# Sigmoid by way of the hyperbolic tangent, and one-number activations beside the square root, in a four-layer graph network

## The chip, the cores and the metric

The kernel runs on one core of a Trainium2 chip. The core has engines that work side by side, each with its own queue of instructions in a fixed order: TensorE (PE, matrix products), VectorE (DVE), ScalarE (ACT, functions and copies), GpSimd (POOL) and SyncE (SP, which here only issues transfers). The metric is device time in microseconds (us) from start to end; lower is better. Three runs of the kernel before took 5743.28, 5758.06 and 5765.65 us; their median, 5758.06 us, is the time before.

## The reference, cut to what matters

There are 16 graphs of 1024 nodes with 64 numbers a node, and an adjacency matrix of 1024 x 1024 each. Four layers follow one another. Each is a residual step that begins with a normalization without learned scale, clipped at zero:

```python
def _layernorm(x, axis=-1, eps=1e-5):
    m = jnp.mean(x, axis=axis, keepdims=True)
    v = jnp.var(x, axis=axis, keepdims=True)
    return (x - m) / jnp.sqrt(v + eps)

h = jnp.maximum(_layernorm(x, axis=-1), 0.0)
x = x + _L0_gnn_ref(h, adj, nodemask, ...)   # quantiles over the neighbours, then a small dense net
# layer 1: message net, A @ m, then a gated update
r = jax.nn.sigmoid(i_r + h_r)
z = jax.nn.sigmoid(i_z + h_z)
n = jnp.tanh(i_n + r * h_n)
return (1.0 - z) * n + z * h
# layer 2: A @ h, dense, tanh, dense        -> x + tanh(...) @ W2 + b2
# layer 3: attention over columns, softmax, weighted sum, relu
```

So one graph needs the square root once at each of four normalizations, the sigmoid and the hyperbolic tangent in layer 1, the hyperbolic tangent in layer 2 and the exponential in layer 3. All of these run on ACT, which evaluates functions from a table that has to be in place. In the trace a change of table is an instruction of its own, ACT_TABLE_LOAD.

## The kernel before, in words

Graphs are worked on in eight pairs. The four layers of the reference are spread over stages, which repeat from pair to pair with a period of some 695 us:

- **Sorting and neighbours.** `sort_begin` (L750) loads the two graphs' node features (`xt`, a buffer of the name `s4` with three places), normalizes them (`norm`, L705, under the name `so`) and transposes them; `sort_pair` (L778) sorts each channel on DVE and works the ranks backwards; `prepare` (L1617) calls `neighbours` (L882), which reads the adjacency, thins out the edges and writes a transposed copy of the adjacency to HBM (`a_d`).
- **Selection.** `weights` (L984) and `select` (L1105) find the quantiles of layer 0, for both graphs of the pair, with matrix products, sign functions and maxima. No square root, tangent or exponential occurs there.
- **Leftovers.** `extras` (L1325) treats the rows that the selection could not settle.
- **Layers.** `layers` (L1398) does the rest of layer 0 and layers 1 to 3 for one graph. It is called for both graphs of the pair (names `ly0` and `ly1`), and each call contains three normalizations under the name `ly`.

While the layers of one pair run, `prepare` and `sort_pair` for the next pair, and `sort_begin` for the pair after that, are offered beside them. In the last pair there is nothing to put beside the layers.

The order on each engine's queue is not written by hand. A planner takes the instructions in the order in which the program states them as their rank, walks through a modelled time with its own costs, and at each moment gives an engine the highest-ranked instruction that is ready in that model. So the first graph's layers rank above the second's, both above `prepare` and `sort_pair`, and `sort_begin` ranks last. The queue that comes out is fixed: on the chip an engine whose next instruction waits does not go on to a later one. The table loads are put in afterwards, when the queue's order is known: one stands ahead of each activation whose function the table in place does not serve.

The parts that the change touches:

- In `norm`, DVE takes statistics of each group of 64 numbers (L710) and combines them (L712), eight groups for a graph, sixteen for a pair; ACT takes the square root into `sd` (L714); DVE inverts it (L716), subtracts the mean (L718), and clips and scales (L720). L718 does not need `sd`, L716 and L720 do.
- In `layers`, the gates of layer 1 are made for two node groups at a time: PE writes the products to a bank of PSUM (L1535), ACT takes the sigmoid of the first two gates into `rz` (L1540), DVE multiplies the first gate into the candidate's hidden part and adds the input part (L1542, L1543). After four such rounds ACT takes the hyperbolic tangent of all candidates (L1544), and four DVE instructions blend it with `h1` and add the residual (L1546 to L1549).
- Layer 2 takes its hyperbolic tangent at L1560. Layer 3 loops over eight blocks of the adjacency: a scaled copy on ACT (L1587), a minimum on DVE (L1589) with two one-column helpers (L1592, L1593), the exponential on ACT (L1595), a masked sum on DVE (L1596), a scaling of the features on ACT (L1601), and the product on PE (L1485). The exponentials are written to `att`, which has two places.

Of the kernel before, what the change touches and what calls it, by code (L numbers as in the profile page):

```python
# [9 lines left out]
F32 = mybir.dt.float32  # L10
# [7 lines left out]
AF = mybir.ActivationFunctionType  # L18
ALU = mybir.AluOpType
# [23 lines left out]
def gnn_stack(ctx, tc, x, adj, nodemask, w, out):  # L43
# [10 lines left out]
    nc = tc.nc  # L54
    B, N, C = x.shape
# [17 lines left out]
    eps = const.tile([P, 1], F32, name="eps")  # L73
# [630 lines left out]

    def norm(pool, big, xt, g, name):  # L705

        st = pool.tile([P, g, 6], F32, name=f"{name}_st")
        mv = pool.tile([P, g, 2], F32, name=f"{name}_mv")
        for t in range(g):
            nc.vector.bn_stats(st[:, t, :], xt[:, t, :])  # L710
        for t in range(g):
            nc.vector.bn_aggr(mv[:, t, :], st[:, t, :])  # L712
        sd = pool.tile([P, g], F32, name=f"{name}_sd")
        nc.scalar.activation(sd, mv[:, :, 1], AF.Sqrt, bias=eps, scale=1.0)  # L714
        rs = pool.tile([P, g], F32, name=f"{name}_rs")
        nc.vector.reciprocal(rs, sd)  # L716
        d = big()
        nc.vector.tensor_sub(d, xt, mv[:, :, 0:1].to_broadcast([P, g, C]))  # L718
        h = big()
        nc.vector.scalar_tensor_tensor(  # L720
            h, d, 0.0, rs.rearrange("p (g o) -> p g o", o=1).to_broadcast([P, g, C]), op0=ALU.max, op1=ALU.mult
        )
        return h
# [674 lines left out]
    def layers(b, side_, agg, ly, lb, held=None):  # L1398
# [5 lines left out]
        def nd(name, bufs=1):  # L1404
            return ly.tile([P, NT, C], F32, name=name, bufs=bufs)

        def big():
            return nd("nd", 4)
# [4 lines left out]
        def bank():  # L1413
            return lb.tile([P, HALF], F32, name="bank")
# [31 lines left out]
        def add_row(po, row_3):  # L1446

            n = row_3.shape[1]
            nc.tensor.matmul(
                po.rearrange("p (t c) -> p t c", c=n), ones_3,  # L1450
                row_3.rearrange("k (o c) -> k o c", o=1).to_broadcast([3, HALF // n, n]), start=True, stop=False,
            )
# [60 lines left out]


        h1 = norm(ly, big, x1, NT, "ly")
        hT = transposed(h1, "hT")
        both_ = ly.tile([P, 2, HALF], F32, name="two")
# [11 lines left out]
        rz = ly.tile([P, N], F32, name="att", bufs=2).rearrange("p (t k) -> p t k", k=2 * C)  # L1529
        nn = big()  # L1530
        for g in range(0, NT, 2):
            pg = bank()
            add_row(pg, gates_3)
            for f in range(2):
                nc.tensor.matmul(  # L1535
                    pg[:, f * 4 * C : (f + 1) * 4 * C], both_[:, f, g // 2 * P : (g // 2 + 1) * P], gates[:, f, :],
                    start=False, stop=(f == 1),
                )
            pg = pg.rearrange("p (t k) -> p t k", k=4 * C)
            nc.scalar.activation(rz[:, g : g + 2, :], pg[:, :, : 2 * C], AF.Sigmoid)  # L1540
            rn = ly.tile([P, 2, C], F32, name="rn", bufs=2)
            nc.vector.tensor_mul(rn, rz[:, g : g + 2, :C], pg[:, :, 3 * C :])  # L1542
            nc.vector.tensor_add(nn[:, g : g + 2, :], rn, pg[:, :, 2 * C : 3 * C])  # L1543
        nc.scalar.activation(nn, nn, AF.Tanh)  # L1544
        x2 = nd("xs", 2)
        nc.vector.tensor_sub(x2, h1, nn)  # L1546
        nc.vector.tensor_mul(x2, x2, rz[:, :, C:])
        nc.vector.tensor_add(x2, x2, nn)
        nc.vector.tensor_add(x2, x2, x1)  # L1549


        h2 = norm(ly, big, x2, NT, "ly")
        h2T = transposed(h2, "srcT")
        pm = bank()
# [90 lines left out]
    for pr in range(pairs):  # L1645
# [17 lines left out]
        with ExitStack() as beside:  # L1663
# [14 lines left out]
            with (  # L1678
                tc.tile_pool(reuse_waits="tile", name="ly0", bufs=1) as ly0,
                tc.tile_pool(reuse_waits="tile", name="ly1", bufs=1) as ly1,  # L1680
                tc.tile_pool(reuse_waits="tile", name="lb0", bufs=4 if final else 3, space=PSUM) as lb0,
                tc.tile_pool(reuse_waits="tile", name="lb1", bufs=4 if final else 2, space=PSUM) as lb1,
                ExitStack() as besides,
            ):
                if not final:
                    sop = besides.enter_context(tc.tile_pool(reuse_waits="tile", name="sop", bufs=1, space=PSUM))
                for i, (ly, lb) in enumerate(((ly0, lb0), (ly1, lb1))):
                    layers(pr * 2 + i, (pr * 2 + i) % 4, aggs[i], ly, lb, held[i])
                if pr + 1 < pairs:
                    made = prepare(pr + 1, nb, nbp)  # L1690
                    sort_pair(pr + 1, cur, sop)
                if pr + 2 < pairs:
                    cur = sort_begin(pr + 2, sop)
# [47 lines left out]
```

## Time and profile before

| | |
|---|---|
| median of three runs | 5758.06 us |
| the profiled execution, its own time | 5775.25 us |
| its span | 5773.4 us |
| busy: DVE / PE / ACT | 4997.9 / 4354.5 / 3813.2 us |
| table loads on ACT | 91, of 1283 ns each |
| square roots (L714) | 56: 8 of `so`, 48 of `ly` |
| a selection stage, 2382 to 2763 us | DVE 355.3, PE 329.2, ACT 279.7 us busy of 381 |
| a stage of leftovers, layers and sorting, 2062 to 2382 us | DVE 263.4, PE 214.1, ACT 197.7 us busy of 320 |
| last layers alone, 5597 to 5773.4 us | PE 118.6, DVE 83.0, ACT 79.1 us busy of 176.4 |

The times are from one execution recorded by the hardware profiler. "Busy" leaves out register, branch, semaphore and transfer-issuing instructions. In lists of groups a line gives source line, engine, operation, output<-input by the program's names, shapes and count, then the total busy time and the mean of one instruction in nanoseconds, and last the engine's idle time just before these instructions with what ended it. The chain of waits is followed back from the last instruction: at each step to what released it or to the instruction before it on its engine; its lines give start, duration, engine, output and source line, and "issue" is time in which an engine waited for nothing that the profile shows. A table load has no output, so in the chain it appears as an engine and a line alone, or inside an "issue".

### The profile page before, as it was taken

Reading aid. Unit: us, or ns where it says so; the run is one execution under the profiler, and the core shown is the slowest. Engines: PE = TensorE matmul, PEld = TensorE weight load, DVE = VectorE, ACT = ScalarE, POOL = GpSimd, SP = SyncE. Lnnn points to the kernel's source line nnn. Section 1 sums busy time; section 2 is a strip of 40 time slices with the busy share of each in tenths; the row PEclk is TensorE's granted clock in tenths of the full one; section 3 lists DMA queues with packets and bytes.
Section 4 is the critical chain, followed back from the end, with each engine's and each line's share of the span. In section 5 each row is a group of like instructions: output and inputs, shape, how many; then the busy total and the mean of one; then the engine's idle time right before and its main releaser. Section 6 shows DMA issues by size and latency. Waiting matters only on the chain.

```text
span 5773.4 us, 114332 instructions
## 1 busy us (share of the span) xinstructions
PE 4354.5 (75%) x45010; PEld 2724.9 (47%) x45010; DVE 4997.9 (87%) x13239; ACT 3813.2 (66%) x5763; POOL 166.5 (3%) x292
## 2 busy tenths in 40 slices
PE   1488677886778957788588885788767886779956
PEld 1355443554435544455434554355543554435642
DVE  9899888998889987999879988799888998878754
ACT  2587657775586855868568666687667866477835
POOL 3000000000000000000000000000000000000000
PEclk9699878997789978899779996899868997789967
DMA  4401264013731047210561115611255013630030
GB/s 129 127 27 41 88 208 134 26 37 107 227 96 35 28 133 232 68 37 23 158 225 53 41 45 175 199 38 40 82 173 173 28 40 90 212 113 18 10 101 5
DMA packets 519813, 551.45 MB, mean 96 GB/s; under 512 B 263297, under 2 KB 413057, under 8 KB 519265
## 3 DMA queue, kind: packets, MB, share of 16 engines
q1 hardware_dynamic: 376864, 459.65, 25.5%
q10 hardware_dynamic: 140064, 81.84, 4.6%
q8 instruction: 355, 5.82, 0.4%
q0 software_dynamic: 2336, 2.57, 0.2%
q14 instruction: 194, 1.58, 0.1%
HBM read 360.17 MB, written 183.76 MB: 94 GB/s over the span
## 4 chain that ended last, share of the span: by engine, by line
PE 34%; DVE 32%; ACT 19%; DMA 10%; issue 4%; POOL 0%; SPq 0%; ACTq 0%; DVEq 0%; POOLq 0%
PE comb L1120 11%; ACT sign L1175 6%; DVE y L1191 5%; PE cand L1220 5%; PE comb L1311 3%; PE bank L1485 3%; DVE cand L1228 3%; DMA a_d<-at 2%; ACT y L1128 2%; DVE cum L902 2%; DMA adjT<-a_d 2%; DVE s L793 1%; DVE s L792 1%; PE pk L952 1%; DVE swapped L791 1%
## 5 line engine op out<-in xcount | busy, mean ns | idle before, releaser
L1120 PE MATMUL comb<-wt,ndT 128*128 128x512 fp8e5 x6144 | 1435.6, 385 | 136.3 <-ACT sign L1175 112.1
L1128 ACT ACTIVATE y<-comb,qb 128x512 int16<-128x512 f32 x1152 | 743.5, 711 | 497.2 <-PE comb L1120 497.2
L1120 PEld LDWEIGHTS <-ndT 128*128 128x128 fp8e5 x6144 | 589.3, 98 | 852.9 <-issue 222.2
L1175 ACT ACTIVATE sign<-comb,lower 128x1024 fp8e5<-128x1024 int16 (+1 forms) x640 | 694.1, 1085 | 0.0
L1175 ACT ACTIVATE sign<-comb,half 128x1024 fp8e5<-128x1024 int16 (+1 forms) x640 | 688.9, 1076 | 0.0
L1220 PE MATMUL cand<-vtab,sign 128*128 128x48 f16 (+1 forms) x18432 | 668.4, 191 | 25.1 <-DVE agg L1097 15.2
L1220 PEld LDWEIGHTS <-sign 128*128 128x128 fp8e5 x18432 | 641.7, 96 | 85.1 <-issue 23.9
L1191 DVE TENSOR_TENSOR y<-y 128x512 uint16<-128x512 uint16 (+5 forms) x896 | 670.1, 790 | 10.5 <-PE comb L1173 10.0
L1228 DVE COPY_PREDICATED cand<-w_f,cand 128x256 f32<-128x256 uint16 (+1 forms) x1536 | 532.7, 378 | 84.1 <-PE cand L1220 81.7
L1173 PE MATMUL comb<-ident_b,y 128*128 128x128 bf16 x4608 | 307.0, 218 | 102.2 <-ACT sign L1175 70.2
L910 ACT COPY at<-pk 128x512 f32<-128x512 f32 x256 | 147.2, 585 | 351.6 <-PE pk L908 177.2
L952 PE MATMUL pk<-minus_b,rem 128*128 128x128 bf16 x1024 | 231.4, 251 | 175.6 <-ACT rem L933 175.6
L1173 PEld LDWEIGHTS <-y 128*128 128x128 bf16 x4608 | 284.8, 97 | 127.2 <-issue 127.1
L952 PE MATMUL pk<-ident_b,ni 128*128 128x128 bf16 x1024 | 227.0, 247 | 108.0 <-ACT ndT L958 63.4
L902 DVE TENSOR_TENSOR_SCAN cum<-ni 128x1024 f16<-128x1024 fp8e5 x128 | 292.3, 2284 | 17.7 <-POOL ni L898 14.4
L1485 PE MATMUL bank<-att,hs 128*64 128x512 f32 x512 | 195.7, 876 | 143.5 <-ACT hs L1601 143.5
L908 PE MATMUL pk<-ident,a 128*128 128x128 f32 x1024 | 188.0, 330 | 144.8 <-DMA a<-in_adj_dram 92.0
L998 DVE TENSOR_SCALAR wt<-node 128x2048 uint8<-128x2048 f16 x224 | 263.3, 1219 | 21.9 <-PE comb L1311 21.9
L1485 PE MATMUL bank<-adjT,nd 128*64 128x512 f32 x896 | 255.5, 638 | 29.7 <-DMA adjT<-a_d 29.2
L792 DVE TENSOR_TENSOR s<-s 128x384 f32<-128x384 f32 (+4 forms) x440 | 263.2, 598 | 0.0
L793 DVE TENSOR_TENSOR s<-s 128x384 f32<-128x384 f32 (+4 forms) x440 | 262.1, 596 | 0.0
L1186 DVE TENSOR_SCALAR y<-y 128x4608 int16<-128x4608 int16 x128 | 173.6, 1356 | 97.6 <-ACT y L1128 96.7
(382 smaller groups left out, 8340.5 us busy)
## 6 DMA issues: line engine op xcount, KB each, us to landing
adjT<-a_d SPq DMA_DIRECT2D x336, 512.0 KB
a<-in_adj_dram SPq DMA_DIRECT2D x128, 512.0 KB
a_d<-at ACTq DMA_DIRECT2D x256, 256.0 KB
m_d<-swapped SPq DMA_DIRECT2D x104, 512.0 KB
swapped<-m_d SPq DMA_DIRECT2D x104, 512.0 KB
n_d<-nat SPq DMA_DIRECT2D x128, 128.0 KB
x_d<-xr SPq DMA_DIRECT2D x48, 256.0 KB
comb_x<-x_d ACTq DMA_DIRECT2D x24, 512.0 KB
```

The lines of the kernel that those rows point to most:

```text
L792: nc.vector.tensor_tensor(to_lo, lo, hi, op=ALU.max)
L793: nc.vector.tensor_tensor(to_hi, lo, hi, op=ALU.min)
L902: nc.vector.tensor_tensor_scan(cum[:, t - t0, :], ni[:, t, :], wide[:, t, pad - 1 : pad - 1 + N], 0.0, op0=ALU.add, op1=ALU.add)
L952: nc.tensor.matmul(pk[:, n % 4, :], lhs, rhs, start=(n % 4 == 0 and m == 0), stop=(m == len(terms) - 1 and last),)
L1120: nc.tensor.matmul(pw, ndT[:, j, t * P : (t + 1) * P], wt[1 + g8][:, j].rearrange("p w c -> p (w c)"), start=(j == 0), stop=(j == NT - 1),)
L1128: nc.scalar.activation(y[:, 0, chunks, at : at + 8 * d_].rearrange("p q (w d) -> p q w d", d=d_), pw.rearrange("p (w q d) -> p q w d", w=8 ...
L1173: nc.tensor.transpose(pt[:, q - q0, :], y[:, 0, q, :].bitcast(BF16), ident_b)
L1175: nc.scalar.activation(signs[tl][s][:, q0:q1, :], pt.bitcast(I16), AF.Sign, bias=before[s], scale=-1.0, saturate=False,)
L1191: nc.vector.tensor_tensor(v[:, :, :, :n], v[:, :, :, :n], v[:, :, :, n : 2 * n], op=ALU.max)
L1220: nc.tensor.matmul(cand[:, e, at : at + 12 * d_].rearrange("p (d l) -> p d l", l=12), signs[tl][sec][:, chunk, :], tab[:, q, :, half_ * 12 ...
L1228: nc.vector.copy_predicated(v[:, :, :, dst : dst + k], mk.to_broadcast([P, 2, C // 2, k]), v[:, :, :, frm : frm + k])
L1485: nc.tensor.matmul(po[to : to + C, :], lhs, rhs[:, f * HALF : (f + 1) * HALF], start=(j == 0), stop=(j == NT - 1))
```

## The change

The sigmoid is written as half of one plus the hyperbolic tangent of half the argument. ACT now computes the tangent with a scale of 0.5 at L1540, and `rz` holds the tangents. The half and the one go into the DVE instructions that follow: two `tensor_tensor` forms at L1542 and L1543 become `scalar_tensor_tensor` (add one, multiply; multiply by a half, add), and two of the four that blend (L1547, L1548) likewise. The number of DVE instructions stays what it was.

In `norm` two ACT instructions on a single number are added, with results that nothing reads, in a tile `turn` of one partition and two numbers. The first is a square root (scale 0, so that its value doesn't depend on its input); it reads the first number of `xt` and stands ahead of the statistics. The second is an exponential, also with scale 0; it reads the first number of `sd` and stands right after the square root. This concerns all 56 normalizations, in `sort_begin` and in `layers`.

```diff
     def norm(pool, big, xt, g, name):
 
+        turn = pool.tile([1, 2], F32, name=f"{name}_turn")
+        nc.scalar.activation(turn[:, :1], xt[:1, 0, :1], AF.Sqrt, bias=eps[:1], scale=0.0)
         st = pool.tile([P, g, 6], F32, name=f"{name}_st")
...
         sd = pool.tile([P, g], F32, name=f"{name}_sd")
         nc.scalar.activation(sd, mv[:, :, 1], AF.Sqrt, bias=eps, scale=1.0)
+        nc.scalar.activation(turn[:, 1:], sd[:1, :1], AF.Exp, scale=0.0)
         rs = pool.tile([P, g], F32, name=f"{name}_rs")
...
-            nc.scalar.activation(rz[:, g : g + 2, :], pg[:, :, : 2 * C], AF.Sigmoid)
+            nc.scalar.activation(rz[:, g : g + 2, :], pg[:, :, : 2 * C], AF.Tanh, scale=0.5)
             rn = ly.tile([P, 2, C], F32, name="rn", bufs=2)
-            nc.vector.tensor_mul(rn, rz[:, g : g + 2, :C], pg[:, :, 3 * C :])
-            nc.vector.tensor_add(nn[:, g : g + 2, :], rn, pg[:, :, 2 * C : 3 * C])
+            nc.vector.scalar_tensor_tensor(rn, rz[:, g : g + 2, :C], 1.0, pg[:, :, 3 * C :], op0=ALU.add, op1=ALU.mult)
+            nc.vector.scalar_tensor_tensor(
+                nn[:, g : g + 2, :], rn, 0.5, pg[:, :, 2 * C : 3 * C], op0=ALU.mult, op1=ALU.add
+            )
         nc.scalar.activation(nn, nn, AF.Tanh)
         x2 = nd("xs", 2)
         nc.vector.tensor_sub(x2, h1, nn)
-        nc.vector.tensor_mul(x2, x2, rz[:, :, C:])
-        nc.vector.tensor_add(x2, x2, nn)
+        nc.vector.scalar_tensor_tensor(x2, rz[:, :, C:], 1.0, x2, op0=ALU.add, op1=ALU.mult)
+        nc.vector.scalar_tensor_tensor(x2, x2, 0.5, nn, op0=ALU.mult, op1=ALU.add)
         nc.vector.tensor_add(x2, x2, x1)
```

## The prediction

> **What bounds the kernel now.** I read the page first, then the busy times by stage, then the table loads among ACT's groups, then the chain of waits around them, and last ACT's own order in an attention stretch. Busy times, of the whole span and of four stretches (length, busy time with count per engine, granted clock, share of the DMA engines, GB/s):
>
> ```profile
> PE 4354.5 (75%) x45010; PEld 2724.9 (47%) x45010; DVE 4997.9 (87%) x13239; ACT 3813.2 (66%) x5763; POOL 166.5 (3%) x292
> ...
> 2382.00:2763.00 381.00, 329.16 (x3931) 211.67 (x3930) 355.30 (x923) 279.71 (x456) 2.92 (x5) 0.95 0.12 36
> ...
> 2062.00:2382.00 320.00, 214.12 (x1698) 126.48 (x1699) 263.39 (x724) 197.74 (x266) 12.46 (x23) 0.74 0.58 180
> ...
> 2305.00:2382.00 77.00, 50.81 (x304) 23.02 (x304) 63.87 (x197) 62.41 (x84) 0.00 (x0) 0.73 0.38 104
> ...
> 5597.00:5773.40 176.40, 118.59 (x435) 56.48 (x434) 82.99 (x270) 79.05 (x107) 2.88 (x4) 0.70 0.06 13
> ```
>
> Selection (second line) is DVE's, 93% busy, and has no changed instruction. Everything changed lies in the third kind of stretch, which comes seven times, and in the last one. Nothing is full there: ACT is at 62%, DVE at 82%. Inside it the attention loops (fourth line) have ACT at 81% and DVE at 83%. So a microsecond on ACT counts only where the chain passes through ACT. ACT's groups (x count | busy us, mean ns):
>
> ```profile
> L714 ACT ACT_TABLE_LOAD x45 | 57.7, 1283 | 7.3 <-DVE ly_mv L712 4.7 <-issue 1.9
> ...
> L1540 ACT ACT_TABLE_LOAD x16 | 20.5, 1283 | 0.3
> L1595 ACT ACT_TABLE_LOAD x16 | 20.5, 1283 | 0.3
> ...
> L1560 ACT ACT_TABLE_LOAD x13 | 16.7, 1283 | 0.2
> L714 ACT ACTIVATE ly_sd<-ly_mv,eps 128x8 f32<-128x8 f32 x48 | 14.4, 300 | 8.3 <-DVE ly_mv L712 7.9
> ...
> L851 ACT CAST wtab<-ends 128x11 f16<-128x11 f32 x16 | 3.2, 203 | 0.0
> L1291 ACT COPY vx<-comb 64x9 f32<-64x9 f32 x16 | 2.6, 162 | 25.3 <-DVE who L1290 25.2
> ...
> L1544 ACT ACT_TABLE_LOAD x1 | 1.3, 1283 | 0.0
> ```
>
> The five kinds of load are 91, or 91 x 1.283 = 116.8 us of ACT. Only part of that stands in the chain of waits (start, duration, what):
>
> ```profile
> 2278.44 1.28 ACT L714
> ...
> 2321.58 1.02 issue
> ...
> 5655.39 1.28 ACT L714
> ...
> 5674.18 1.09 issue
> ...
> 5675.59 1.28 ACT L1544
> ...
> 5734.67 1.28 ACT L1595
> ```
>
> The "issue" of 2321.58 is the load of L1595 that ran from 2321.30; that of 5674.18 is one of L714. Going through all 91 in this way, 21.5 us of loads lie on the chain: 6.4 in the last layers, and 1.2 to 3.5 in each of the seven stages before. That is the most that moving loads can take off this chain directly.
>
> **The change, part by part.**
>
> *Arithmetic on DVE: 0.* L1542 and L1543 are now 281 and 280 ns as products and sums from PSUM; the scalar_tensor_tensor of L1097, also from PSUM, has 277 ns for 64 columns against the 278 ns of L1095's simpler form. At 128x512, L720 (scalar_tensor_tensor) has 688 ns against the 686 of L1547 and L1548. The 160 rewritten instructions move by at most 10 ns each, 1.6 us in all, either way.
>
> *The tangent in the sigmoid's place: the 17 loads at L1540 and L1544 go.* L1544 takes a tangent right after L1540's sigmoids without a load in 15 of 16 cases, and L1595 follows the tangent of L1560 without one (5711.00, then 5712.02): a tangent is served by the sigmoid's table and by the exponential's. But L1560's table doesn't serve L1540: at 5668.46 there is a load between them. Afterwards only two tables remain, one for the root and one for the rest. The activation itself costs the same within its row, 383 ns at 128x256 (the copy-like L958 has 379).
>
> *Loads after.* Each of 56 normalizations asks for the root's table and then for the other: 112 against 91, so 21 x 1.283 = 26.9 us more, if nothing comes between the one-number root and the real one.
>
> *What comes between.* The first one-number root is ready when `xt` is, the real one after eight statistics and combinations (1.10 + 0.62 us, less where they overlap: 1.66 us). In an attention loop ACT has exponentials of the other graph to give out meanwhile. In ACT's order at 2315:
>
> ```profile
> 2315.70 1.24 ACT L1595 ACTIVATE att<-adjT,top 128x1024 f32<-128x1024 f32 x1
> 2316.85 1.13 ACT L1587 ACTIVATE adjT<-adjT,fdst 128x1024 f32<-128x1024 f32 x1
> ...
> 2319.45 1.28 ACT L714 ACT_TABLE_LOAD   x1
> 2320.74 0.30 ACT L714 ACTIVATE ly_sd<-ly_mv,eps 128x8 f32<-128x8 f32 x1
> ...
> 2321.30 1.28 ACT L1595 ACT_TABLE_LOAD   x1
> ```
>
> `xs` is complete at 2314.1. A root placed there brings its table, the exponential of 2315.70 brings the other back, and 2319.45 needs the root's again: two loads more for one normalization. This holds for the third normalization of the second graph in seven stages, and for the six `so` that fall into attention loops (as at 2370.26): there the first graph's features are asked for at 2327.98 and the root runs 42 us later, with some ten exponentials between. So 13 places, 26 reloads, 33.4 us of ACT. Their number has 0 as its floor (the planner keeps each pair together) and three or four places a pair as a ceiling, about 28 places.
>
> *The one-number activations.* No row has one. The root with a pointer for its bias is nearest to L714, 300 ns for eight columns: 0.29 us. The exponential lies between 162 (L1291) and 300 ns: I take 0.21, by L851 and its eleven columns. Together 56 x 0.50 = 28 us of ACT, at least 56 x 0.32 = 18, at most 34.
>
> *The added wait.* The one-number root waits for `xt`; behind it in ACT's queue stand the other graph's exponentials and the evictions of `prepare` (L910, L958), and for these DVE and PE wait. For `ly` the wait is one for DVE that ends 1.66 us before the old one. For `so` it is one for a transfer: if the first graph's alone counts, its 2327.98 leaves 21 us until the statistics of 2349.14, and the wait is nothing; if the second's too (2356.01, statistics at 2360.74), at most 4.7 us, six times 28 us. I take 0, as the number read is the first graph's. SP and POOL issue nothing new.
>
> *What leaves the path.* Loads on the chain that get a cover: 904.08, 3003.46, 4391.18, 5087.08, 2278.44, 5655.39 and 5734.67, 7 x 1.28 = 9.0 us. The first four and the last go under the transposes and products that follow the square root; the other two go under the statistics. What is late next there is the root itself, behind DVE's L712. Seven L1595 loads (7.4 us) and that of L1544 stay, because the one-number exponential takes them at the same place in the queue; three L714 loads (915.38, 5673.98, 5696.43; 3.9 us) stay, since other functions stand before them.
>
> *What comes onto the path.* Each of the 13 places pushes ACT back by load, root and reload, 1.28 + 0.29 + 1.28 = 2.86 us, and the idle gaps of ACT in such a loop are at most 1.44 us, so at least half remains: 13 x 1.43 = 18.6 us. The rest, 26.9 + 28.0 - 13 x 0.29 = 51.1 us, is spread over stretches where ACT has 13% of the chain (42.2 of 324.6 us from 2062): 6.6 us.
>
> *Sum.* -9.0 + 18.6 + 6.6 = +16.2 us. On the profiled execution's 5775.25 us that gives 5791.5; this execution stood 17.2 us above the median of 5758.06, so against the runs I expect 5774.3.
>
> A rule against the change: the Trainium skill's page "ScalarE: Activation LUTs" (Table sets) says to batch calls by set and to do all of one before switching; one-number calls that ask for tables ahead do the opposite wherever two graphs share the queue. The same page (What ACT_TABLE_LOAD costs) puts a switch at 2.66 us with a drain; here the load takes 1.283 us and the root starts 1.29 us after it, so the trace decides. By the page's figure the 26 reloads would cost 18 us more on the path, an estimate of 5792.
>
> **The rivals.**
>
> *Faster.* All of the 21.5 us leave the chain, and the second graph's queueing shrinks too: in the last layers its statistics end at 5685.44 and its root waits until 5697.72 behind the first graph's attention, 12.3 us. If the new order lets it through, 5758.06 - 21.5 - 12.3 = 5724. For it speaks that the last layers are one dependent chain with ACT at 45%; against it, that first-graph work still outranks it, and that two instructions more ask for room.
>
> *Slower, on the other side.* ACT becomes the bound of the attention loops. The new work is 26.9 + 33.4 + 28.0 = 88 us of ACT; it decides once more than 38 us of that (43%) lie on the path, as 38 - 9 is 0.5%. At 60%, since ACT is 81% busy there: 53 - 9 = +44, 5802. For it speaks that DVE gets its exponentials from ACT one at a time (two places of `att`); against it, that DVE holds 52% of the chain in that stretch and ACT 11%.
>
> *It doesn't do what it says.* The one-number root lands right before the real one, as rank order would put it on a busy ACT: no lead and no reload. Then 26.9 + 28.0 = 55 us of ACT at 13% is +7, 5765.
>
> **How the numbers follow.** A difference under 0.5%, 29 us, can't be told from none by runs that spread over 22 us. Forecast, reloads half hidden: 0.40, with 5755 to 5790 as its own range. No effect: 0.08. Slower: 0.35. Faster: 0.17. So within 0.5% 0.48, slower 0.35, faster 0.17. The range leaves out a tenth at each end: from 5725, the faster rival's, to 5820, which is 9.0 off and four fifths of the 88 us on the path. As one planned order is repeated in six stages, an accident of 3 us comes six times; this is why I don't go narrower.
>
> **What would show it.** Right: about 112 + 26 = 138 loads, 0 at L1540 and L1544, ACT near 3901 us, DVE within 2 us, loads of L714 and L1595 alternating around 2310 to 2370, none on the chain at L1560. Fewer than 115 loads would refute the reloads; a chain without loads and stages shorter by over 3 us would make the faster rival right. The prediction fails if the planner's new order moves `prepare` or the transfers of `adjT` against the layers, which no row of before can show.

## The result, and the profile after

The changed kernel takes 5817.54 us (median of 4 runs, 5811.38 to 5832.02) against 5761.85 us (median of 4, 5743.28 to 5774.27) for the kernel before in the same comparison: 1.0104 times as long, 95% interval 1.0083 to 1.0125. The forecast was 5774 us and "within 0.5%". The time lies inside the given range, but the change is slower, by about 56 us.

The profiled execution of the changed kernel took 5820.4 us, its span is 5818.5. Its busy times, from the page:

```profile
PE 4353.4 (75%) x45010; PEld 2730.1 (47%) x45010; DVE 5000.5 (86%) x13239; ACT 3896.1 (67%) x5926; POOL 172.5 (3%) x292
```

Four stretches of it (length, busy time with count per engine, granted clock, share of the DMA engines, GB/s), set at the same distance from the square roots as those shown of before: selection, a stage with layers, its part with the attention loops, the last layers.

```profile
2400.70:2781.70 381.00, 329.93 (x3938) 212.27 (x3936) 355.69 (x921) 279.74 (x457) 2.92 (x5) 0.96 0.11 35
2076.70:2400.70 324.00, 217.12 (x1698) 130.60 (x1699) 265.18 (x730) 207.90 (x287) 13.81 (x24) 0.73 0.59 180
2319.70:2400.70 81.00, 53.94 (x351) 26.16 (x352) 62.55 (x195) 70.36 (x95) 0.00 (x0) 0.77 0.43 122
5643.10:5818.50 175.40, 118.44 (x439) 56.12 (x439) 83.83 (x273) 88.39 (x124) 2.79 (x4) 0.71 0.06 13
```

Selection is unchanged at 381 us. The stage with layers is 4 us longer, and in the attention loops ACT is busy 70 of 81 us, 87%, where it was 62 of 77. The last layers, where nothing stands beside them, are 1 us shorter although ACT is busy 9 us more there. Measured from the first square root of one stage to that of the next, the seven steps grew by 2.9, 9.7, 3.8, 4.0, 10.4, 6.8 and 6.4 us, 44.0 of the 45.1 us by which the two spans differ (one execution of each kernel; a single step moves by several us between executions, as the tangent run below shows, whose third step took 690.5 us where the kernel before took 699.7 with the same order). So the loss sits in the seven stages in which `prepare` stands beside the layers.

The table loads and the one-number activations among ACT's groups:

```profile
L708 ACT ACT_TABLE_LOAD x56 | 71.8, 1283 | 6.7 <-DMA s<-in_x_dram 4.3 <-DVE xs L1567 1.4
...
L717 ACT ACT_TABLE_LOAD x49 | 62.9, 1283 | 2.3 <-ACT ly_sd L716 1.6
...
L1600 ACT ACT_TABLE_LOAD x20 | 25.7, 1283 | 0.3
...
L716 ACT ACT_TABLE_LOAD x15 | 19.2, 1283 | 0.3
...
L708 ACT ACTIVATE ly_turn<-xs,eps 1x1 f32<-1x1 f32 x48 | 14.1, 293 | 6.2 <-DVE xs L1515 2.9 <-DVE xs L1567 1.8 <-DVE xs L1554 1.2
...
L717 ACT ACTIVATE ly_turn<-ly_sd 1x1 f32<-1x1 f32 x48 | 9.7, 202 | 0.5
...
L1543 ACT ACT_TABLE_LOAD x2 | 2.6, 1283 | 0.0
```

There are 142 loads where 91 were. This bill came out almost as it was forecast (138 loads, 0.29 and 0.21 us, ACT near 3901 us), but the time did not. What also changed is the order of SP's queue. These are SP's transfers in one stage, of the kernel before (start, time over which the group was issued, line, what, count):

```profile
2250.94 1.18 SPq L1478 DMA_DIRECT2D adjT<-a_d  x2
2252.17 2.62 SPq L896 DMA_DIRECT2D a<-in_adj_dram  x2
...
2258.22 19.88 SPq L1478 DMA_DIRECT2D adjT<-a_d  x8
...
2286.42 9.43 SPq L1478 DMA_DIRECT2D adjT<-a_d  x6
```

and of the changed kernel, in the same stage, where the clock of the profile is 14.7 us further on (first square root at 2220.88 instead of 2206.19):

```profile
2270.29 16.25 SPq L1481 DMA_DIRECT2D adjT<-a_d  x9
2286.60 0.90 SPq L899 DMA_DIRECT2D a<-in_adj_dram  x2
...
2288.60 9.90 SPq L1014 DMA_DIRECT2D vtab<-w_d  x7
2308.76 16.39 SPq L1481 DMA_DIRECT2D adjT<-a_d  x11
```

The first square roots of the stage, in ACT's order, of the kernel before and of the changed one:

```profile
2206.19 0.30 ACT L714 ACTIVATE ly_sd<-ly_mv,eps 128x8 f32<-128x8 f32 x1
...
2220.88 0.30 ACT L716 ACTIVATE ly_sd<-ly_mv,eps 128x8 f32<-128x8 f32 x1 [0.45 <-DVE ly_mv L714]
```

Two adjacency loads `a` of the next pair's `prepare` (the last two of its second graph) were issued 46 us after the stage's first square root and are now issued 66 us after it, behind the first adjacency blocks of the first graph's attention. What this does is read from the chain of waits of the changed kernel, some of its pieces in order:

```profile
2286.60 6.74 DMA a<-in_adj_dram
...
2293.38 1.13 PE pk L911 x4
...
2295.02 0.31 ACT ly_sd L716
...
2300.36 2.29 DVE cum L905
2302.65 0.58 DVE nd L723
...
2304.74 2.29 DVE cum L905
...
2319.22 6.98 DMA adjT<-a_d
```

The root of 2295.02, of the first graph's third normalization, stands in ACT's queue behind the copies of the transposed `a`, so it waits for the transfer. Then the two scans of `prepare` (L905, 2.29 us each) stand on DVE around L723 of 2302.65, which finishes the second graph's second normalization. In the chain of the kernel before that step began at 2280.30 (`2280.30 0.70 DVE nd L720`), 74.1 us after the first square root; now it begins 81.8 us after it. PE needs its result to work off the adjacency blocks, whose three buffers then come free later, and the next six to eleven blocks are issued 87.9 instead of 80.2 us after the first root. The second graph's third root falls from 114.5 to 125.7 us. In the sums over the whole run this is PE's group of products with `adjT`, the kernel before,

```profile
L1485 PE MATMUL bank<-adjT,nd 128*64 128x512 f32 x896 | 255.5, 638 | 29.7 <-DMA adjT<-a_d 29.2
```

and the changed one, whose PE waits 23 us longer for these transfers (the tangent run below, with the order of before, has 23.9 us, so this figure moves by some 6 us between executions):

```profile
L1488 PE MATMUL bank<-adjT,nd 128*64 128x512 f32 x896 | 256.5, 640 | 53.0 <-DMA adjT<-a_d 52.6
```

So there were two theories. **Loads:** the 51 added loads and 112 added activations, 83 us more on ACT, take the time (this is the prediction's rival "slower"). **Order:** the planner, which counts loads in its modelled time, laid out the stages anew, and the new order costs the time whatever the loads do.

### The profile page after: what moved, and what is told of

Its sections match the earlier page's. It is cut to its first block, busy times and chain, and to the rows that moved or that the text cites. A ratio compares the mean times of both kernels' runs of the same rounds, so it can differ in the third digit from the quotient of the medians.

```text
span 5818.5 us, 114419 instructions
## 1 busy us (share of the span) xinstructions
PE 4353.4 (75%) x45010; PEld 2730.1 (47%) x45010; DVE 5000.5 (86%) x13239; ACT 3896.1 (67%) x5926; POOL 172.5 (3%) x292
## 4 chain that ended last, share of the span: by engine, by line
PE 35%; DVE 28%; ACT 22%; DMA 10%; issue 4%; POOL 0%; SPq 0%; ACTq 0%; DVEq 0%; POOLq 0%
PE comb L1123 11%; ACT sign L1178 6%; DVE y L1194 5%; PE cand L1223 5%; PE bank L1488 4%; PE comb L1314 4%; DMA adjT<-a_d 3%; DVE cand L1231 3%; ACT y L1131 2%; DVE cum L905 2%; DMA a_d<-at 2%; PE pk L955 1%; ACT att L1600 1%; DMA a<-in_adj_dram 1%; ACT sq L935 1%
## 5 line engine op out<-in xcount | busy, mean ns | idle before, releaser
L905 DVE TENSOR_TENSOR_SCAN cum<-ni 128x1024 f16<-128x1024 fp8e5 x128 | 292.3, 2284 | 10.5 <-POOL ni L901 10.5
L955 PEld LDWEIGHTS <-rem 128*128 128x128 fp8e5 x1024 | 115.8, 113 | 348.6 <-ACT rem L936 190.3
L1488 PE MATMUL bank<-att,hs 128*64 128x512 f32 x512 | 207.7, 898 | 90.4 <-ACT hs L1606 89.9
```

The costliest lines, as they stand in the source:

```text
L905: nc.vector.tensor_tensor_scan(cum[:, t - t0, :], ni[:, t, :], wide[:, t, pad - 1 : pad - 1 + N], 0.0, op0=ALU.add, op1=ALU.add)
L955: nc.tensor.matmul(pk[:, n % 4, :], lhs, rhs, start=(n % 4 == 0 and m == 0), stop=(m == len(terms) - 1 and last),)
L1488: nc.tensor.matmul(po[to : to + C, :], lhs, rhs[:, f * HALF : (f + 1) * HALF], start=(j == 0), stop=(j == NT - 1))
```

## The experiments

Each ratio is to the kernel before in the same comparison, with its 95% interval. The edits are against the changed kernel unless another is named.

**Two by two: order and loads apart.** The tangent alone leaves every queue in the order of before:

```diff
-        turn = pool.tile([1, 2], F32, name=f"{name}_turn")
-        nc.scalar.activation(turn[:, :1], xt[:1, 0, :1], AF.Sqrt, bias=eps[:1], scale=0.0)
...
-        nc.scalar.activation(turn[:, 1:], sd[:1, :1], AF.Exp, scale=0.0)
```

> The tangent in the sigmoid's place alone, without the one-number activations. Every queue holds its instructions in the order of the kernel before; only the forms differ, and the table loads are 90 instead of 91. Loads as the cause (L) and order as the cause (O) both expect the time before within 0.3%, 5745 to 5780 us against 5762. If this part costs by itself (the forms of DVE, the tangent), it would be above 5780.

Measured: 5751.8 us, 0.9998 (0.9981 to 1.0014). The tangent and the rewritten DVE instructions cost and bring nothing that can be measured.

The second kernel takes that one and sets 108 one-number activations into ACT's finished queue, so that the old order has 142 loads (cut; `None` stands for the instruction that was there, `ahead` names the instruction before which a root goes, `behind` the real root):

```diff
+        for i in block.instructions:
+            todo = [(AF.Sqrt, m) for m in ahead.get(i.name, ())] + [None]
+            todo += [(AF.Exp, behind[i.name])] if i.name in behind else []
+            for one in todo:
+                if one is None:
+                    kept.append(i)
+                    continue
...
+                kept.append(mybir.InstActivation(
...
```

> e1 with its order kept in every queue, and 108 one-number activations set into ACT's finished queue: a root ahead of each normalization's root (ahead of the nearest exponential where one lies among the four activations before it, else one place ahead), an exponential behind it. 142 table loads, as many as the changed kernel has. They wait for nothing. L: most of the changed kernel's loss is here, e1 plus 35 to 60 us (5795 to 5825). O: the loads find room, e1 plus 0 to 20 us (5760 to 5785).

Measured: 5831.88 us, 1.0135 (1.0119 to 1.0152), 80 us over the tangent alone and so above what either theory expected.

The third holds the changed kernel's order in every queue and turns its one-number activations into copies after planning, which leaves 79 loads:

```diff
+            if isinstance(i, mybir.InstActivation) and i.func in (AF.Sqrt, AF.Exp) and "_turn" in str(i.outs[0].memref):
...
+                i = mybir.InstActivation(func=AF.Identity, ins=list(i.ins), outs=list(i.outs), **had)
```

> The changed kernel with its order kept in every queue, but after planning the 112 one-number activations are turned into copies that every table serves. 79 table loads instead of 142, so 81 us of ACT less, with the same waits and the same places. L: 63 loads of 1.283 us at 60% or more on the path come off, 5755 to 5775 us. O: the order carries the loss, 5795 to 5820 us.

Measured: 5820.63 us, 1.0115 (1.0098 to 1.0132), and PE waits as long as in the changed kernel:

```profile
L1488 PE MATMUL bank<-adjT,nd 128*64 128x512 f32 x896 | 261.2, 653 | 52.2 <-DMA adjT<-a_d 52.1
```

The new order loses all of it without the loads; inside that order 63 loads fewer bring nothing (1.0115 against 1.0104). The loads theory falls for the changed kernel. But it is no general answer that loads are free: in the old order 52 more loads and the 108 activations (67 + 27 us of ACT) cost 80 us over the tangent alone. Why they cost so much there was not taken apart. The inserted roots end a median of 1.4 us ahead of the real ones, no less than in the changed kernel (1.0 us); but the real roots of the layers start a median of 2.9 us after their last statistics, against 1.8 us with the tangent alone and 0.8 us in the changed kernel, so more stands ahead of them on ACT.

**A different source for the one-number root.** It reads the last group's variance, so that it can't run before the statistics are done:

```diff
-        nc.scalar.activation(turn[:, :1], xt[:1, 0, :1], AF.Sqrt, bias=eps[:1], scale=0.0)
...
+        nc.scalar.activation(turn[:, :1], mv[:1, g - 1, 1:], AF.Sqrt, bias=eps[:1], scale=0.0)
```

> The changed kernel, but the one-number root reads the last of the combined statistics instead of the layer's input, so that it is ready only when the real root is. 114 loads instead of 142: the reloads in between are gone, and the planner makes an order of its own. L: 28 loads or 36 us of ACT less at 60%: about 5795 us. O: wherever the new order falls, 5750 to 5830; what tells is whether the second graph's third normalization comes 114 us after the first graph's first one, as before, or 126 us, as in the changed kernel.

Measured: 5863.47 us, 1.0187 (1.0170 to 1.0204), with 114 loads. Fewer loads than the changed kernel and a longer time, above both expectations. The second graph's third normalization, which was to tell the theories apart, comes later than in either kernel, 132.5 us after the first root in the stage shown (2356.30 against 2223.84); the two adjacency loads are late here too, and PE's wait for adjacency blocks is 65.2 us.

**What moves the order.** The one-number activations stay, but as copies, which need no table, so that the planner counts no loads for them:

```diff
-        nc.scalar.activation(turn[:, :1], xt[:1, 0, :1], AF.Sqrt, bias=eps[:1], scale=0.0)
+        nc.scalar.activation(turn[:, :1], xt[:1, 0, :1], AF.Identity, bias=eps[:1], scale=0.0)
...
-        nc.scalar.activation(turn[:, 1:], sd[:1, :1], AF.Exp, scale=0.0)
+        nc.scalar.activation(turn[:, 1:], sd[:1, :1], AF.Identity, scale=0.0)
```

> The changed kernel with its 112 one-number activations traced as Identity, which needs no table: the same instructions with the same waits, but the planner charges no loads for them. The order that it makes is close to that of the kernel before (second graph's third normalization after three attention blocks of the first, adjacency of the next pair loaded after the first sixteen blocks), and it holds 79 loads. Theory A (the planner moves things because of the loads it charges, and that move is the loss): within 0.5% of the kernel before, 5740 to 5780 us. Rival B (112 more instructions with their waits already cost it): 5800 us or more. My number: 5760, as 112 x 0.25 us = 28 us of ACT against 12 loads fewer, 15 us.

Measured: 5741.59 us, 0.9984 (0.9967 to 1.0001). The adjacency loads are where the kernel before has them, PE waits 23.1 us, and 112 more instructions cost nothing. So it is the loads in the planner's reckoning, not the instructions, that make it choose the new order.

The same plan, and after planning the copies become roots and exponentials:

```diff
+            if isinstance(i, mybir.InstActivation) and i.func == AF.Identity and "_turn" in str(i.outs[0].memref):
...
+                i = mybir.InstActivation(func=AF.Sqrt if i.outs[0].offset == 0 else AF.Exp, ins=list(i.ins), outs=list(i.outs), **had)
```

> The order of the run with copies kept in every queue, and after planning the one-number activations are turned back into roots and exponentials: 156 loads in an order that was made without them. Theory C (loads set into an order that has no room for them land on the path at about 85%, as when they were inserted into the old order): 77 loads more than with copies, 99 us, times 0.85: about 84 us over the run with copies, 5845. Rival D (the inserted ones cost so much only because of where I had put them): at most a third of it, 33 us over, under 5795. Where theory A holds as well, the changed kernel itself (5818) lies between: the planner's move then is the cheaper way out.

Measured: 5792.25 us, 1.0076 (1.0054 to 1.0098), 51 us over the copies for 77 loads (98.8 us). Loads that the plan did not know of cost about half their time here, between theory C's 85% and rival D's third; both were off. The expectation that the planner's own answer would be the cheaper way out was not borne out: 1.0104 with the loads known against 1.0076 without, with intervals that overlap.

**One half of the pair.** The one-number exponentials alone:

```diff
-        nc.scalar.activation(turn[:, :1], xt[:1, 0, :1], AF.Sqrt, bias=eps[:1], scale=0.0)
```

> The change without its 56 one-number roots; the one-number exponentials stay. 112 loads, and no root is ever asked for ahead, so no table is taken from the other graph's exponentials. The planner's order is again a new one: the next pair's scans come after the first graph's later normalizations, and the second graph's third normalization is spread over the first graph's attention blocks six to nine. If the order is what costs (theory A): 5800 to 5830. If the one-number roots with their bringing back of tables are what costs: 5755 to 5785.

Measured: 5788.1 us, 1.0067 (1.0044 to 1.0091), between the two expectations. The adjacency loads are late (PE waits 53.0 us), the loads are 112. It speaks for the order, less clearly than the third kernel.

**The adjacency first.** All adjacency loads of `prepare` get the highest rank:

```diff
-                nc.sync.dma_start(a, adj[b, t * P : (t + 1) * P, :])
+                with tc.high_priority():
+                    nc.sync.dma_start(a, adj[b, t * P : (t + 1) * P, :])
```

> The changed kernel, with the loads of the next pair's adjacency given the highest rank in the plan. All four scans of a stage now stand before the third normalizations as in the kernel before, but the second graph's third normalization falls behind eight attention blocks of the first instead of six (three before). 130 loads. If the late adjacency alone makes the loss (the scans between the second graph's statistics and its attention): 5755 to 5780. If the place of the second graph's third normalization among the attention blocks makes it: 5815 or more. If both are parts of one loss: between.

Measured: 5684.92 us, 0.9896 (0.9872 to 0.9920): faster than either kernel. The third normalization of the second graph is still late (121.2 us after the first root, 2293.31 against 2172.16, behind eight attention blocks), so its late place does not by itself make the loss; PE waits 25.0 us. The gain went beyond what I expected of any theory, so the next runs asked whether it belongs to the change. The same edit in the kernel before:

```diff
-                nc.sync.dma_start(a, adj[b, t * P : (t + 1) * P, :])
+                with tc.high_priority():
+                    nc.sync.dma_start(a, adj[b, t * P : (t + 1) * P, :])
```

> The kernel before, unchanged but for the highest rank of the adjacency loads in the plan, as in the run with the changed kernel: 67 loads of tables against that one's 130. Beside the kernel before at 5750 us. Theory F (the early adjacency helps either kernel by the same, and what the change adds in this place is its loads at about half their time, 63 x 1.283 x 0.5 = 40 us): 5650. Theory G (the planner hides the change's loads where the adjacency is early, so the change costs nothing there): 5690, as the changed kernel with the same edit. Rival H (the gain belonged to the one order that the planner found for the changed kernel, not to the early adjacency): 5740 or more.

Measured: 5728.63 us, 0.9954 (0.9937 to 0.9971). The early adjacency brings the kernel before 0.5%. With it in both, the changed kernel is the faster one, 0.9896 against 0.9954, 33 us, with intervals apart. This lies between theories G and H: about half of the gain is the adjacency's own, the other half comes only with the change, that is, with its loads and with the order that the planner makes for them.

The same with the tangent (this edit on the kernel of the first experiment):

> The same with the sigmoid from the tangent and without the one-number activations: same order in every queue as the run beside it but for one table load less (66). All theories: within 0.3% of that run, since the tangent alone made no difference in the old order. It is the one part of the change that could stay.

Measured: 5729.87 us, 0.9953 (0.9934 to 0.9971), as expected.

**What the one-number calls do when the order is held.** The adjacency first, that plan held, and the one-number activations turned into copies afterwards, as in the third kernel:

> The changed kernel with the adjacency first (5685 us, 130 loads), its order held in every queue, and its one-number activations turned into Identity after planning: 93 loads. Theory G (loads that the planner knew of cost nothing, as with the changed kernel's own order, where 63 loads fewer gave 3 us the other way): 5685, within 10. Theory C (a load costs half its time on the path): 37 x 1.283 x 0.5 = 24 us less, 5660.

Measured: 5717.56 us, 0.9938 (0.9921 to 0.9955). Both theories missed: with 37 loads *fewer* it is 0.42% slower than with them, 24 us, the intervals just apart (0.9920 and 0.9921). So by these medians most of the 33 us comes with the calls that ask for tables, not with the order alone. ACT's order shows what the loads buy. With the one-number root live:

```profile
2169.62 1.28 ACT L708 ACT_TABLE_LOAD   x1
2170.92 0.29 ACT L708 ACTIVATE ly_turn<-xs,eps 1x1 f32<-1x1 f32 x1
...
2172.16 0.28 ACT L716 ACTIVATE ly_sd<-ly_mv,eps 128x8 f32<-128x8 f32 x1
```

and at the same place with a copy instead:

```profile
2176.41 0.28 ACT L708 ACTIVATE ly_turn<-xs,eps 1x1 f32<-1x1 f32 x1
...
2177.75 1.28 ACT L716 ACT_TABLE_LOAD   x1
2179.05 0.30 ACT L716 ACTIVATE ly_sd<-ly_mv,eps 128x8 f32<-128x8 f32 x1
```

The load that stood right ahead of the real root is now ahead of the statistics, so the prefetch does what it says. How the whole 24 us come about is not settled: loads on the chain, counted as in the prediction, are 46.1 us with the prefetch and 50.0 without, which is only 4 of them.

**What all loads are worth.** The tangent alone in the order of before, with the layers' square roots turned into copies after planning, so that 14 loads remain of 90:

```diff
+            if isinstance(i, mybir.InstActivation) and i.func == AF.Sqrt and "ly_sd" in str(i.outs[0].memref):
...
+                i = mybir.InstActivation(func=AF.Identity, ins=list(i.ins), outs=list(i.outs), **had)
```

> The tangent in the order of before, with the 48 square roots of the layers' normalizations turned into Identity after planning, so that they need no table: 14 loads instead of 90. It leaves out part of the computation: the layers are divided by the variance and not by its root. It measures what the table loads of the old order are worth in all, which is the most that any prefetch of them could win. By the chain of waits, on which 17.7 us of loads lay with the tangent alone: 18 us less than that kernel, 5733. By the price found with the loads that were added to the plan blind (51 us for 77, half their time): 76 x 1.283 x 0.5 = 49 us less, 5702.

Measured: 5728.59 us, 0.9958 (0.9935 to 0.9980), 23 us under the tangent alone. With intervals of 0.3 to 0.5% from end to end this is nearer to the 18 us of the chain than to the 49 of the half price: for the loads of the old order, the chain of waits was the better measure.

**The two adjacency loads by themselves.** So far the late adjacency only went along with the loss. In the kernel before, a constraint puts just these two loads late:

```diff
+    fetched = []
...
-            nc.sync.dma_start(t, a_d[side_, j])
+            fetched.append(nc.sync.dma_start(t, a_d[side_, j]).ins)
...
-                nc.sync.dma_start(a, adj[b, t * P : (t + 1) * P, :])
+                with tc.issue_after(fetched[-48 + 18]) if b > 1 and b % 2 and t >= NT - 2 else ExitStack():
+                    nc.sync.dma_start(a, adj[b, t * P : (t + 1) * P, :])
```

> The kernel before, arithmetic and activations unchanged, with one constraint for the plan: the last two adjacency loads of the next pair (row blocks 6 and 7 of its second graph) are issued behind the third adjacency block of the first graph's attention, the place that the changed kernel's plan gave them. Their two scans now stand after the second graph's second normalization, as in the changed kernel; 67 loads of tables against 91. Theory O (the late pair of loads is by itself the loss): PE's wait for adjacency blocks rises from 29 to about 50 us, and the time to 5800 or more, though 24 loads are gone. Rival M (the late pair of loads only goes along with the loss, which comes from the rest of the order, such as the third normalization after six attention blocks): 5735 to 5775.

Measured: 5836.96 us, 1.0145 (1.0120 to 1.0169), with 24 loads of tables fewer than the kernel before and none of the change. The time is what theory O asked for; PE's wait rose to 41.4 us and not to about 50. SP's queue, and PE's group:

```profile
2281.40 12.49 SPq L1481 DMA_DIRECT2D adjT<-a_d  x8
2293.94 0.90 SPq L897 DMA_DIRECT2D a<-in_adj_dram  x2
...
2308.73 30.10 SPq L1481 DMA_DIRECT2D adjT<-a_d  x12
```

```profile
L1488 PE MATMUL bank<-adjT,nd 128*64 128x512 f32 x896 | 245.5, 637 | 41.4 <-DMA adjT<-a_d 41.1
```

Its chain has the two scans and the wait for an adjacency block too, but the scans stand behind both normalizations, and neither the loads `a` nor a root behind them lies on it in this stage:

```profile
2302.64 0.68 DVE nd L720
2303.32 2.20 DVE cum L903
...
2306.74 2.20 DVE cum L903
...
2314.47 5.04 DMA adjT<-a_d
```

And in the changed kernel, just these two loads early:

```diff
-                nc.sync.dma_start(a, adj[b, t * P : (t + 1) * P, :])
+                with tc.high_priority() if b > 1 and b % 2 and t >= NT - 2 else ExitStack():
+                    nc.sync.dma_start(a, adj[b, t * P : (t + 1) * P, :])
```

> The changed kernel with the highest rank for these same two loads alone. The first graph's stages and the scans are then where the kernel before has them, while the second graph's third normalization stays behind six attention blocks, as in the changed kernel; 128 loads of tables. Theory O: the loss of 60 us is gone, 5750 or less with a PE wait for adjacency blocks under 35 us. Rival M: 5800 or more. If the first run stays near before and this one comes down, the two loads matter only where the layers' roots are asked for ahead.

Measured: 5736.23 us, 0.9967 (0.9951 to 0.9982), with 128 loads. The loss is gone, and a third of a percent with it; whose gain that is, the change's or the rank's, is not known, since the kernel before was run only with all adjacency loads first. SP's queue has the two loads back, and PE's wait is the one of before:

```profile
2234.14 5.91 SPq L1482 DMA_DIRECT2D adjT<-a_d  x4
2240.31 3.52 SPq L900 DMA_DIRECT2D a<-in_adj_dram  x2
2243.89 19.25 SPq L1482 DMA_DIRECT2D adjT<-a_d  x11
```

```profile
L1489 PE MATMUL bank<-adjT,nd 128*64 128x512 f32 x896 | 244.5, 634 | 29.1 <-DMA adjT<-a_d 28.7
```

Two transfers put late, with the plan that the planner makes around them, bring a loss where nothing else of the change is; put early they take it away where all else of the change stays. All kernels in one table, by the place of these two loads:

| the two loads | kernel | table loads | PE's wait for `adjT`, us | ratio |
|---|---|---|---|---|
| as before | before | 91 | 29.7 | 1 |
| as before | tangent only | 90 | 23.9 | 0.9998 |
| as before | copies | 79 | 23.1 | 0.9984 |
| as before | no layer roots | 14 | 23.0 | 0.9958 |
| as before | loads set into the old order | 142 | 21.8 | 1.0135 |
| as before | loads set into the plan of the copies | 156 | 19.7 | 1.0076 |
| late | changed | 142 | 53.0 | 1.0104 |
| late | changed order, copies | 79 | 52.2 | 1.0115 |
| late | root reads the statistics | 114 | 65.2 | 1.0187 |
| late | exponentials only | 112 | 53.0 | 1.0067 |
| late | before, two loads late | 67 | 41.4 | 1.0145 |
| early | changed, two loads early | 128 | 29.1 | 0.9967 |
| early | before, all adjacency first | 67 | 25.9 | 0.9954 |
| early | tangent, all adjacency first | 66 | 27.3 | 0.9953 |
| early | changed order, copies, adjacency first | 93 | 32.9 | 0.9938 |
| early | changed, all adjacency first | 130 | 25.0 | 0.9896 |

Every kernel with the late loads is slower than before, with any number of table loads; of the others only those two are into whose finished queues loads were put. What stays open is how the loss divides between the transfer that holds up ACT's queue, the scans on DVE and the later adjacency blocks; they come one after another from the same two loads and were not taken apart, and no run moved the two loads alone in a finished queue. PE's wait is a mark of the state, not its size: 12 to 36 us more of it go with 38 to 108 us. The constraint and the rank also moved other instructions of the plan, so the two runs show the effect of the loads' place with what the planner makes of it.

## Why the prediction was wrong

**What bounds the kernel:** right. The loss lies in the stretches named, selection did not move, the last layers changed by 1 us. (The shares of the chain in the attention stretch, given as 52% for DVE and 11% for ACT, come out as 50% and 12% from 2305 to 2382; nothing hangs on it.)

**Arithmetic on DVE, 0 within 1.6 us:** right as far as the runs can tell. DVE is at 5000.5 us against 4997.9, and at 4996.0 with the tangent alone, whose time is 0.9998.

**Loads, reloads, one-number activations:** right in the count, 142 for 138 (15 reloads at the real root where 13 were expected), 293 and 202 ns for 290 and 210, ACT at 3896.1 us for 3901. Two loads remain at L1543, where none were expected. That ACT's total is so near is partly luck: four loads more than forecast add 5 us, while the one-number activations add 17.5 us of busy time (3896.1 less 142 loads, against 3813.2 less 91) and not 28, because they overlap with their neighbours; below, the instruction behind the root of 2341.07 starts at 2341.27, before its 0.29 us are over. The reload in the attention loop stands exactly as described, from ACT's order:

```profile
2341.07 0.29 ACT L708 ACTIVATE ly_turn<-xs,eps 1x1 f32<-1x1 f32 x1
2341.27 0.33 ACT L1606 ACTIVATE hs<-hh,top 128x64 f32<-128x64 f32 x1
2341.62 1.28 ACT L1600 ACT_TABLE_LOAD   x1
2342.91 2.37 ACT L1600 ACTIVATE att<-adjT,top 128x1024 f32<-128x1024 f32 x2
2345.30 1.28 ACT L716 ACT_TABLE_LOAD   x1
2346.60 0.30 ACT L716 ACTIVATE ly_sd<-ly_mv,eps 128x8 f32<-128x8 f32 x1
```

**The added wait, 0:** on ACT it is small, as forecast: 4.3 us of idle time in all ahead of the loads at L708 until a transfer of node features (`<-DMA s<-in_x_dram`), where at most 28 were allowed. But a wait was looked for on ACT alone; "SP and POOL issue nothing new" was true of the instructions and taken for true of their order.

**What leaves the path, 9.0 us, under a ceiling of 21.5:** the ceiling holds within the interval; without the layers' roots 23 us are gained in the old order. The prefetch itself is worth nothing in the changed order (1.0104 with it, 1.0115 without) and 24 us with the adjacency first. In the changed kernel's trace loads on the chain went up instead, from 23.0 to 42.3 us when one count is made over both, and this goes with the order: by the same kind of count the kernel with the changed order and 79 loads still has some 40.

**What comes onto the path, 18.6 + 6.6 us:** this is where ACT's added time was priced. With the plan made blind, half of a load's time does land on the path, 51 us for 98.8, the rate assumed for the 13 places; the 13% assumed for the rest was too low. So the sum would have missed even with the adjacency loads in their old place: that kernel, with 156 loads, 18 more than forecast, is 44 us above the kernel before (1.0076), where the sum has 16.2. But in the changed kernel that price is not paid as such at all, since the same order without the loads is no faster.

**The step that failed** first is not one of these terms but their frame: the sum took the edited kernel as the kernel before with other instructions in the same order. It ended at +16.2 us; the order it left out is worth about +66 us with the loads taken away again (1.0115), and +80 us when the late place of the two adjacency loads is put into the kernel before. The prediction named this as its condition for failing ("moves `prepare` or the transfers of `adjT` against the layers"), and gave it neither a price nor a chance of its own. Rows of before pointed there: PE already waited 29.2 us for adjacency blocks, and `prepare`'s loads share their queue. They give no size, since the runs show no fixed ratio between that wait and the time.

**The rivals.** "Slower" had 5802, a chance of 0.35 and the wrong mechanism: the same order without the added loads is as slow. "Faster" (all 21.5 us leave, and the second graph's queueing shrinks) did not happen. A gain of that size appears with the adjacency first, where the change is worth 33 us, but not by that mechanism: 46.1 us of loads still lie on the chain there, and the last layers take as long, 148.9 us from their first root to the end against 148.6 without the change.

**The rule that spoke against the change.** The Trainium skill, "ScalarE: Activation LUTs" (Table sets), says to gather calls by table set. The runs agree where loads come unplanned (1.0076 and 1.0135) and disagree where the order leaves room for them, with the adjacency first: there the kernel that switches 130 times beats the same order with 93. The same page puts a switch at about 1.28 us of load and 1.38 us of drain; after loads at L708 the traces have the load's 1283 ns and the next activation mostly within 70 ns of its end (with the adjacency first: load at 2169.62, activation at 2170.92, and 2290.07, 2291.41), so no run here shows the drain.

## What to carry to other kernels

Where a planner fixes the queues, an edit of cheap instructions is an edit of its costs: before pricing the edit, list the transfers that other work waits for and ask what a different order would do to each, and after it, compare the order of every queue, SP's first. Hold the order and take the instructions out, and hold the instructions and change the order: two runs tell which of the two costs. Judge a prefetch in more than one order; here the same 112 one-number calls cost 1.0% in the order the planner found and, with one rank added for the adjacency, belong to the fastest kernel of all, 1.04% faster than before.

## What the runs showed that was not expected

- Two transfers of 512 KB a stage, issued some 20 us later in SP's queue, cost 80 us over seven stages, 11 us each, with the plan that was made around them (1.0145).
- 112 one-number copies on ACT cost nothing measurable (0.9984), although ACT is 81% busy in the attention loops of the kernel before. Beside the table loads they add some 16 us to its busy time (3814.2 us with 79 loads, against 3811.9 with 90 for the tangent alone).
- A table load is a fixed 1283 ns in every kernel here, but its price on the path ran from less than nothing (24 us slower *without* 37 of them) over a quarter (23 us for 76 in the old order) and half (51 us for 77, planned blind) to most of it (80 of 94 us, set into the finished order of before; the 94 hold 27 us of one-number activations).
